# Two-layer graph and mixture-of-experts kernel: fillers of layer 0's table on SyncE, adjacency tiles held per pass, 25 pairs of pages in flight, four rounds of pages first

## The chip, the core and the metric

The kernel runs on one core of one Trainium2 chip. A core has five engines with a queue each: TensorE (PE, with its weight loads as PEld), VectorE (DVE), ScalarE (ACT), GpSimd (POOL) and SyncE (SP). SP computes nothing here: it issues DMAs. ACT and POOL issue some too. The metric is the device time of one execution in microseconds. Before the change it is 1949.97 us, the median of three runs (1948.76 to 1953.71).

## The reference

The input is x with 128 graphs of 64 nodes and 256 features, which is 8192 tokens, and an adjacency matrix of 64 x 64 for each graph. Two layers follow one another, each a graph step and a mixture of experts:

```python
x = x + _L0_gnn_ref(_layernorm(x, axis=-1), adj, ...)
x = x + _L0_ffn_ref(_layernorm(x, axis=-1), L0_ffn_gate_w, L0_ffn_lattice_weights, ...)
x = x + _L1_gnn_ref(_layernorm(x, axis=-1), adj, ...)
x = x + _L1_ffn_ref(_layernorm(x, axis=-1), L1_ffn_Wg, L1_ffn_W1, L1_ffn_W2, ...)
```

The part that matters here is the mixture of layer 0. Each token chooses 6 of 64 experts, an expert is one matrix of 256 x 256, and the token's answer is the sum of its six products, weighted by a softmax:

```python
logits = jnp.einsum('bsd,ed->bse', x, gate_w)
top_logits, indices = jax.lax.top_k(logits, TOP_K)      # TOP_K = 6
scores = jax.nn.softmax(top_logits, axis=-1)
xW = jnp.einsum('bsd,bskde->bske', x, lattice_weights[indices])
lattice_out = jnp.einsum('bske,bsk->bse', xW, scores)
```

Then follow a projection with `out_w`, a residual and a layer norm. Layer 1 multiplies the normed tokens by the adjacency again, and its mixture chooses 2 of 8 experts with a hidden layer of 512.

## The kernel before

Tokens are worked in 32 blocks of 256. There are four stages.

**First stage** (lines 775 to 1069). The graph step of layer 0 for each block, its routing, and a scatter of each token's six rows into a table in DRAM, `r0x`, in which each expert has chunks of its own (`Router.send`, line 419, an indirect DMA of POOL per 128 rows). A row carries 256 numbers, the place where its answer belongs, and its weight. `page_table` (line 443) then lists the pages: a page is 128 rows of one expert. Per expert the first `R` full pages come first, then the other full pages, then parts. The expert matrices, `lat`, are loaded in this stage too and fill 128 KB of each partition.

**Expert stage of layer 0** (lines 1073 to 1215). Twelve pages whose place is known early are done first (`early`). Then pages go in pairs: 188 pairs of listed pages, then 7 pairs whose pages are made of two halves of different experts. Three functions make a pair:

- `fetch(j)`, line 1138: SP loads two pages into `px`, of which there are `bufs=22`. A room comes free when the answers that were written over it have been scattered.
- `flip(j)`, line 1153: PE transposes into `pt` (line 1159), and ACT copies to `pxT` (line 1162).
- `apply(j)`, line 1173: for the first 64 pairs it first calls `r0.fill_end(j)`; then PE multiplies by the matrix (line 1188), DVE weighs the result into `px` (line 1192), and `reply` scatters it by an indirect DMA of POOL into `r0y` (line 426), one for each page.

`staggered` (line 658) sets the program order: a fetch stands 12 pairs ahead of the apply, a transpose 3 pairs ahead (2 for the first four and for the halves). PE, DVE and ACT follow the program order. SP's and POOL's queues are put in order by the framework's scheduler. The framework also has each DMA that SP or ACT issues wait for an earlier DMA on the same one of eight completion lanes.

The fillers: a filler is a page of rows without a token, written behind the last row of an expert so that a part page has defined rows (`fill_end`, line 613, `fill`, line 233; one DMA of 129 KB for each of 64 experts; every fourth call loads four row numbers into registers of the issuing engine). A page that is certainly full is read without waiting for any filler (`full_pages`, 309 pages; pairs from 154 on wait for all fillers).

**Third stage** (lines 1340 to 1667). For each block: the six answers of each token are loaded from `r0y` (`load_y`, line 1355, three rooms `y`), added up by PE (line 1382), projected, normed, and taken through the graph step of layer 1. `READY = 6`: `r0.look_back()` notes after block 5 how many rows each expert has, and `page_table` checks that these all lie in the first `R` pages; then `load_y` of blocks 0 to 5 needn't wait for the answers of later pages (the group `r0last`, which holds the replies from page `R * E` on). Otherwise the kernel runs its spare pages and a wait. `y` uses memory that `lat` leaves.

`load3` (line 1369) loads x and the adjacency of a block. The four adjacency tiles `at0` to `at3` are used in turn by the first and the third stage (`load_adjacency`, line 745). They live in the pool `const` for the whole kernel, 4 KB of each partition, and POOL zeroes them once.

**Fourth stage** (from line 1670). The experts of layer 1 over their pages; its fillers are issued by ACT through the same `fill_end`.

Of the kernel before, what the change touches and what calls it, by code (L numbers as in the profile page):

```python
# [19 lines left out]
P = 128  # L20
# [86 lines left out]
class Router:  # L107
# [502 lines left out]
                                       op0=ALU.add, op1=ALU.max)  # L610
        v.tensor_copy(self.total_pages, most)

    def fill_end(self, e):

        if e % 4 == 0:
            _, self.ends = self.nc.values_load_multi_w_load_instructions(
                self.last[0:1, e:e + 4], engines=[ENG.Activation], min_val=0, max_val=self.spare - self.pg,
                skip_runtime_bounds_check_because="the rows of an expert end in its chunk")
        self.fill(self.nc.scalar, self.ends[e % 4])

    def load(self, what, i, engine):

# [44 lines left out]
def two_layer_gnn_moe_kernel(ctx: ExitStack, tc: tile.TileContext, a: dict, out: bass.AP):  # L667
# [13 lines left out]
    K0 = 6  # L681
    E1, F1, _ = a["L1_ffn_W2"].shape
    EARLY = 12
    READY = 6
    FIRST = 4
    FOLD = 2
    LOOK = 20
# [49 lines left out]


    adjacency = []
    for i in range(4):  # L740
        at = const.tile([P, T, P], F32, name=f"at{i}")
        nc.gpsimd.memset(at, 0.0)
        adjacency.append(at)

    def load_adjacency(b):
        at = adjacency[b % 4]
        for g in range(2):
            nc.sync.dma_start(out=at[g * G:(g + 1) * G, :, g * G:(g + 1) * G],
                              in_=adjT[2 * b * T + g:2 * (b + 1) * T:2].rearrange("t m n -> m t n"))
        return at  # L750
# [24 lines left out]
    with tc.tile_pool(name="c0", bufs=1) as c0, \  # L775
            tc.tile_pool(name="work0", bufs=2) as work, \
            tc.tile_pool(name="ph0", bufs=4, space=PSUM) as ph_pool, \
            tc.tile_pool(name="ps0", bufs=2, space=PSUM) as psum, \
            tc.tile_pool(name="pm0", bufs=1, space=PSUM) as pmix:
        mean = c0.tile([P, P], F32, name="mean")  # L780
        nc.gpsimd.memset(mean, 1.0 / H0)
        route = pmix.tile([P, 2, T, E0], F32, name="route")
# [191 lines left out]
        aggregate(0)  # L974
        rest = lambda f: lambda b: f(b) if b else None

        r0 = Router(tc, const, small, dram, N, D, E0, K0, T, P, 14 * P, 4, "r0", 3, ((K0 * N // P - EARLY) // 4 * 4 + 4, E0 // 2 - 4), True)
        r1 = Router(tc, const, small, dram, N, D, E1, 2, T, 2 * P, N, 4, "r1", 1,
                    (N // P // 2 - E1 // 2, E1 // 4, E1 - 1), True, total=out, like=r0)
        assert W == r0.W  # L980
# [135 lines left out]
    with tc.tile_pool(name="wx0", bufs=3, reuse_waits="tile") as wx, \  # L1116
            tc.tile_pool(name="pt1", bufs=4, space=PSUM, reuse_waits="tile") as pt_pool, \
            tc.tile_pool(name="py1", bufs=4, space=PSUM, reuse_waits="tile") as py_pool:
        npair = (r0.pages + 1) // 2
        pairs = [dict(n=min(2, r0.pages - 2 * j), parts=1) for j in range(npair)]  # L1120
        pairs += [dict(n=2, parts=2) for j in range(E0 // 4)]
        regs = {}
        ring = [wx.tile([P, KD, C], F32, name="pxT", bufs=5)]
        over = dict(ln_g=r0.map.rearrange("p j e -> p (j e)")[:, :D], ln_b=r0.nth.rearrange("p j e -> p (j e)")[:, :D],
                    gamma=r0.end[:, :KD], beta=r0.delta[:, :KD], bg=r0.alloc[:, :E1], gbias=r0.none[:, :E1])

        def load_vectors(j):

            if 8 <= j < 14:
                name, v = (("ln_g", "L0_ffn_ln_g"), ("ln_b", "L0_ffn_ln_b"), ("gamma", "L1_gnn_ln_gamma"),  # L1130
                           ("beta", "L1_gnn_ln_beta"), ("bg", "L1_ffn_bg"), ("gbias", "L1_ffn_bias"))[j - 8]
                with nc.allow_non_contiguous_dma(reason="small vector"):
                    nc.scalar.dma_start(out=over[name], in_=a[v].rearrange("(c p) -> p c", p=P) if j in (10, 11)
                                        else rows_of(a[v]))
            if j == 18:
                nc.vector.tensor_add(over["bg"], over["bg"], over["gbias"])

        def fetch(j):
            Q = pairs[j]
            Q["px"] = px = wx.tile([P, 2, W], F32, name="px", bufs=22)  # L1140
            if j >= npair:
                regs["row"] = r0.load(2, 4 * (j - npair), ENG.SP)
                for i in range(4):
                    q, h = i // 2, i % 2 * P // 2
                    r0.fetch_rows(regs["row"][i], px[h:h + P // 2, q:q + 1, :], P // 2)
                return
            for q in range(Q["n"]):
                i = 2 * j + q
                if i % 4 == 0:
                    regs["row"] = r0.load(0, i, ENG.SP)  # L1150
                r0.fetch(i, regs["row"][i % 4], px[:, q:q + 1, :])

        def flip(j):
            Q = pairs[j]
            pt = pt_pool.tile([P, KD, C], F32, name="pt")
            n = Q["n"]
            for q in range(n):
                for k in range(KD):
                    nc.tensor.transpose(pt[:, k, ts(q, P)], Q["px"][:, q, ts(k, P)], ident)  # L1159
            if Q["parts"] == 1:  # L1160
                Q["xT"] = xT = ring.pop() if ring else wx.tile([P, KD, C], F32, name="pxT", bufs=5)
                nc.scalar.copy(xT[:, :, :n * P], pt[:, :, :n * P])  # L1162
                return
            Q["xT"] = []
            for q in range(n):
                xT = wx.tile([P, KD, C], F32, name="pxT", bufs=5)
                Q["xT"].append(xT)
                nc.vector.memset(xT[:, :, P // 2:P + P // 2], 0.0)
                for h in (0, 1):
                    nc.scalar.copy(xT[:, :, 3 * h * P // 2:3 * h * P // 2 + P // 2],  # L1170
                                   pt[:, :, q * P + h * P // 2:q * P + h * P // 2 + P // 2])

        def apply(j):
            Q = pairs[j]
            if j < E0:
                r0.fill_end(j)
            Q = pairs[j]
            if Q["parts"] == 2:
                regs["e"] = r0.load(3, 4 * (j - npair), ENG.PE)
            elif j % 2 == 0:  # L1180
                regs["e"] = r0.load(1, 2 * j, ENG.PE)
            py = py_pool.tile([P, 2, D], F32, name="py")
            px, xT, n, parts = Q["px"], Q["xT"], Q["n"], Q["parts"]
            for q in range(n):
                for h in range(parts):
                    e = regs["e"][2 * q + h if parts == 2 else (2 * j + q) % 4]
                    for k in range(KD):
                        nc.tensor.matmul(py[:, q, :], lhsT=xT[q][:, k, ts(h, P)] if parts == 2 else xT[:, k, ts(q, P)],  # L1188
                                         rhs=lat[:, ds(e, 1), k, :].rearrange("p o d -> p (o d)"),
                                         start=(h + k == 0), stop=(h == parts - 1 and k == KD - 1))  # L1190
            for q in range(n):
                nc.vector.tensor_scalar(px[:, q, :D], py[:, q, :], px[:, q, D + 1:D + 2], None, op0=ALU.mult)  # L1192
                r0.reply(2 * j + q, px[:, q, :], px[:, q, :D])


        stages = ((-12, fetch), (0, apply),
                  (-2, lambda j: flip(j) if j < 4 or j >= npair else None),
                  (-3, lambda j: flip(j) if 4 <= j < npair else None))

        def run(order, *more):  # L1200
            order = tuple(order)
            staggered(len(order), [*((lag, lambda n, f=f: f(order[n])) for lag, f in stages), *more])

        usual = r0.likely_pages // 2
        likely = (r0.likely_pages + E0 // 8) // 4 * 2
        ends = npair + r0.likely_halves // 4
        run((*range(usual), *range(npair, ends)), (0, load_vectors))
        wait = const.tile([1, 4], F32, name="wait")
        with tc.If(r0.needed(2 * usual)):
            run((*range(usual, likely), *range(ends, len(pairs))))  # L1210
            with tc.If(r0.needed(2 * likely)):
                run(range(likely, npair))

                nc.sync.dma_start(out=wait, in_=r0.answer[0:1, 0:4])
# [125 lines left out]
    with tc.tile_pool(name="c3", bufs=1, reuse_waits="tile") as c3, \  # L1340
# [5 lines left out]
        ln_g, ln_b, gamma, beta, bg = (over[x] for x in ("ln_g", "ln_b", "gamma", "beta", "bg"))  # L1346
        w_rel, w_root = (c3.tile([P, KD, D], F32, name="m_" + x) for x in ("rel", "root"))
        wg = load_matrix(c3, "L1_ffn_Wg")
        one = c3.tile([P, P], F32, name="one")
        nc.vector.memset(one, 1.0)  # L1350
        blocks = [dict() for _ in range(NB)]
# [44 lines left out]
        def fold(b):  # L1396

            B = blocks[b]
            B["n"] = K0
            if b > READY + 1:  # L1400
                B["n"] = n = K0 - FOLD
                y = B["y"]
                nc.vector.tensor_add(y[:, :, :FOLD], y[:, :, :FOLD], y[:, :, n:])
# [266 lines left out]
    with tc.tile_pool(name="pt4", bufs=2, space=PSUM, reuse_waits="tile") as pt_pool, \  # L1670
# [7 lines left out]
        def finish(i):  # L1678
            if i >= 0:
                what, m, new = listed(i)  # L1680
                if i < E1:
                    r1.fill_end(i)
                if new and not (what == 0 and i % 2):
                    regs["e", what] = r1.load(what + 1, m, ENG.PE)
            share(i)
# [61 lines left out]
```

## Time and profile before

| what | us |
|---|---|
| median of the runs | 1949.97 |
| the profiled execution | 1948.88 |
| its span, first to last instruction | 1947.1 |
| PE busy in the span | 1845.0 |
| POOL busy | 1134.5 |
| DVE busy | 1146.9 |
| ACT busy | 1001.6 |
| early answers' scatters on POOL begin | 614.9 |
| first px load, first px scatter | 619.4, 630.2 |
| PE's last product of the expert stage ends | 1097.6 |
| POOL's last scatter of the expert stage ends | 1131.4 |
| PE's last product of the kernel ends | 1931.0 |

Times within the span are counted from its first instruction. The page cuts the span into 40 slices of 48.7 us and gives a busy tenth for each. Windows give the same in stretches that one chooses, with the number of instructions in brackets. A timeline names each instruction with its start, its length, its line, what it writes and reads, and in square brackets the engine's idle time before it and what ended it. The engine's name with a q (SPq) is its queue: there a DMA's line shows its issue, not its transfer. The mean granted clock of PE over the span is 0.98.

### The profile page before, as it was taken

What the parts mean: (1) busy time and instruction counts of PE and PEld (TensorE: products, weight loads), DVE (VectorE), ACT (ScalarE), POOL (GpSimd) and SP (SyncE); (2) the same over time, 40 slices, a digit from 0 to 9 for tenths busy, and PEclk for the clock granted to TensorE, in tenths of its full rate; (3) what the DMA queues carried; (4) which work ended last, traced back from release to release, by engine and by line L of the source; (5) the groups of instructions that cost most, each with busy time, mean ns of one, the idle gap of its engine ahead of it and who ended that gap; (6) DMA issues with size and microseconds to landing.
All of it is one profiled execution on the core that took longest, in us unless ns stands there. A gap on an engine that the chain in (4) does not pass through costs nothing. (4 is left out here: it accounts for less than half of the span.)

```text
span 1947.1 us, 35284 instructions
## 1 busy us (share of the span) xinstructions
PE 1845.0 (95%) x9906; PEld 1608.8 (83%) x9906; DVE 1146.9 (59%) x4256; ACT 1001.6 (51%) x2047; POOL 1134.5 (58%) x1114
## 2 busy tenths in 40 slices
PE   7999999999966898999999899999999999999996
PEld 6888888888844787888887788888888888888885
DVE  5899999999976333344433279999974222222221
ACT  5888898889841222222222156666663333333332
POOL 1377777777677677777777734444454544444443
PEclk9999999999977999999999999999999999999998
DMA  5134555544376988766666689878626766656653
GB/s 141 62 132 144 165 162 164 162 152 137 122 251 193 305 265 263 227 210 204 210 208 201 234 325 328 300 262 287 212 101 139 167 143 127 142 125 141 123 108 44
DMA packets 253085, 359.49 MB, mean 185 GB/s; under 512 B 53176, under 2 KB 210504, under 8 KB 252880
## 3 DMA queue, kind: packets, MB, share of 16 engines
q1 hardware_dynamic: 175904, 210.74, 36.9%
q0 software_dynamic: 62736, 135.21, 23.5%
q10 hardware_dynamic: 14240, 11.12, 1.8%
q8 instruction: 90, 1.47, 0.3%
q14 instruction: 115, 0.94, 0.2%
HBM read 193.27 MB, written 166.03 MB: 185 GB/s over the span
## 5 line engine op out<-in xcount | busy, mean ns | idle before, releaser
L419 POOL DMA_INDIRECT r0x<-xs,r0row x384 | 388.5, 1012 | 215.1 <-ACT lat L883 112.5
L426 POOL DMA_INDIRECT r0y<-px x390 | 378.7, 971 | 122.9 <-issue 40.0
L1188 PE MATMUL py<-lat,pxT 128*128 x1616 | 387.0, 384 | 20.8 <-ACT pxT L1162 17.6
L436 POOL DMA_INDIRECT out_x<-px x131 | 202.8, 1548 | 265.9 <-DVE px L1333 173.7
L1192 DVE TENSOR_SCALAR px<-py,px 128x256 f32<-128x256 f32 x390 | 170.8, 480 | 304.6 <-PE py L1188 298.4
L1188 PEld LDWEIGHTS py<-lat,pxT 128*128 128x128 f32 x1616 | 294.0, 192 | 61.2 <-ACT pxT L1162 23.9
L1162 ACT COPY pxT<-pt 128x512 f32<-128x512 f32 x188 | 109.7, 585 | 346.5 <-PE pt L1159 242.4
L1294 ACT ACTIVATE phid<-ph,pw 128x256 f32<-128x256 f32 (+1 forms) x264 | 122.0, 462 | 287.8 <-PE ph L1285 181.0
L419 POOL DMA_INDIRECT r1x<-xs,r1row x128 | 135.0, 1054 | 179.6 <-ACT hn L1447 55.9
L894 PE MATMUL ps<-lat 128*128 128x256 f32 x1024 | 238.9, 382 | 0.0
L858 PE MATMUL ph<-lat 128*128 128x256 f32 x1024 | 231.5, 385 | 3.2 <-DVE lat L881 2.0
L1310 PE MATMUL py<-fw,phid 128*128 (+1 forms) x1016 | 230.4, 380 | 0.0
L1285 PE MATMUL ph<-pxT,pw 128*128 128x256 f32 (+1 forms) x1056 | 227.3, 368 | 1.5 <-DVE px L1327 1.5
L858 PEld LDWEIGHTS ph<-lat 128*128 128x128 f32 x1024 | 195.0, 193 | 29.6 <-issue 2.7
L894 PEld LDWEIGHTS ps<-lat 128*128 128x128 f32 x1024 | 193.7, 192 | 27.8
L1285 PEld LDWEIGHTS ph<-pxT,pw 128*128 128x128 f32 x1056 | 193.2, 190 | 26.3 <-DVE px L1327 1.9
L1310 PEld LDWEIGHTS py<-fw,phid 128*128 128x128 f32 x1016 | 188.2, 190 | 22.5
L1321 DVE TENSOR_SCALAR p<-p 128x2 f32<-128x2 f32 (+1 forms) x69 | 12.6, 183 | 208.0 <-ACT p L1320 208.0
L1159 PE MATMUL pt<-ident,px 128*128 128x128 f32 x780 | 121.4, 276 | 7.0 <-DMA px<-r0x 6.7
L1327 DVE TENSOR_TENSOR px<-py,pb 128x512 f32<-128x512 f32 (+1 forms) x67 | 44.5, 664 | 138.3 <-PE py L1310 133.7
L881 DVE SCALAR_TENSOR_TENSOR lat<-ph,c_L_gnn_b,rms 128x256 f32<-128x256 f32 x256 | 111.9, 477 | 23.3 <-ACT rms L72 23.3
L1159 PEld LDWEIGHTS pt<-ident,px 128*128 128x128 f32 x780 | 97.5, 142 | 31.5 <-DMA px<-r0x 6.2
(337 smaller groups left out, 2959.6 us busy)
## 6 DMA issues: line engine op xcount, KB each, us to landing
y<-r0y SPq DMA_DIRECT2D x64, 768.0 KB
px<-r0x SPq DMA_DIRECT2D x376, 129.0 KB
pw<-in_L_ffn_W1b SPq DMA_DIRECT2D x41, 514.0 KB
x<-x SPq DMA_DIRECT2D x64, 256.0 KB
px<-r1x SPq DMA_DIRECT2D x28, 516.0 KB
r0x<-r0filler ACTq DMA_DIRECT2D x64, 129.0 KB
lat<-in_x SPq DMA_DIRECT2D x32, 256.0 KB
lat<-in_L_ffn_lattice_weights SPq DMA_DIRECT2D x8, 1024.0 KB
```

What stands on the lines that cost most here:

```text
L419: i = self.nc.gpsimd.indirect_dma_start(out=self.table[:, :], out_offset=bass.IndirectOffsetOnAxis(ap=row[:, t, k:k + 1], axis=0), in_=xs[ ...
L426: d = self.nc.gpsimd.indirect_dma_start(out=self.answer[:, :], out_offset=bass.IndirectOffsetOnAxis(ap=x[:, self.D:self.D + 1].bitcast(I32 ...
L436: i, d = f"{self.name}add{i}", self.nc.gpsimd.indirect_dma_start(out=self.total[:, :], out_offset=bass.IndirectOffsetOnAxis(ap=x[:, self.D ...
L858: nc.tensor.matmul(ph[:, c, :], lhsT=w1[:, k, ts(2 * j + c, P)], rhs=B["aggT"][:, k, :], start=(k == 0), stop=(k == KD - 1))
L881: nc.vector.scalar_tensor_tensor(hT[:, c, :], B["ph", c // 2][:, c % 2, :], b1[:, c:c + 1], B["rms"], op0=ALU.add, op1=ALU.mult)
L894: nc.tensor.matmul(B["po"][:, t, :], lhsT=B["hT"][:, c, ts(t, P)], rhs=w2[:, c, :], start=False, stop=(t == T - 1 and c == KH - 1))
L1159: nc.tensor.transpose(pt[:, k, ts(q, P)], Q["px"][:, q, ts(k, P)], ident)
L1188: nc.tensor.matmul(py[:, q, :], lhsT=xT[q][:, k, ts(h, P)] if parts == 2 else xT[:, k, ts(q, P)], rhs=lat[:, ds(e, 1), k, :].rearrange("p ...
L1192: nc.vector.tensor_scalar(px[:, q, :D], py[:, q, :], px[:, q, D + 1:D + 2], None, op0=ALU.mult)
L1285: nc.tensor.matmul(Q["up", c][:, :m], lhsT=Q["w"][:, k * F1 + c * P:k * F1 + (c + 1) * P], rhs=Q["xT"][:, k, :m], start=(k == 0), stop=(k ...
L1294: nc.scalar.activation(Q["hid"][:, c, :m], Q["up", c][:, :m], AF.Relu, bias=Q["w"][:, KD * F1 + c:KD * F1 + c + 1], scale=1.0)
L1310: nc.tensor.matmul(py[:, t, :], lhsT=Q["hid"][:, c, ts(t, P)], rhs=fw2[:, ds(e, 1), c, :].rearrange("p o d -> p (o d)"), start=(c == 0), s ...
```

## The change

Five things are changed together:

1. Layer 0's fillers are issued by SP within `fetch`, at even pairs from 24 to 150 in program order, in place of ACT within `apply`. Layer 1's stay on ACT.
2. The four adjacency tiles are made twice, in a pool of the first stage (zeroed by POOL) and in a pool of the third (zeroed by DVE), and don't exist in between.
3. `px` has 25 rooms, not 22.
4. `R` of layer 0's router is 4, not 3, so that the list begins with up to four full pages of each expert, and `READY` is 8, not 6.
5. The test for adding up four products in place of six (`fold`) is written with a constant of its own; it is true for the same blocks as before.

```diff
-    def fill_end(self, e):
+    def fill_end(self, e, engine, issuer):
 
         if e % 4 == 0:
             _, self.ends = self.nc.values_load_multi_w_load_instructions(
-                self.last[0:1, e:e + 4], engines=[ENG.Activation], min_val=0, max_val=self.spare - self.pg,
+                self.last[0:1, e:e + 4], engines=[engine], min_val=0, max_val=self.spare - self.pg,
                 skip_runtime_bounds_check_because="the rows of an expert end in its chunk")
-        self.fill(self.nc.scalar, self.ends[e % 4])
+        self.fill(issuer, self.ends[e % 4])
...
-    READY = 6
+    READY = 8
+    WHOLE = 8
...
     adjacency = []
-    for i in range(4):
-        at = const.tile([P, T, P], F32, name=f"at{i}")
-        nc.gpsimd.memset(at, 0.0)
-        adjacency.append(at)
+
+    def clear_adjacency(pool, engine):
+        for i in range(4):
+            at = pool.tile([P, T, P], F32, name=f"at{i}")
+            engine.memset(at, 0.0)
+            adjacency.append(at)
 
     def load_adjacency(b):
-        at = adjacency[b % 4]
+        at = adjacency[b % 4 - 4]
...
+        clear_adjacency(c0, nc.gpsimd)
         mean = c0.tile([P, P], F32, name="mean")
...
-        r0 = Router(tc, const, small, dram, N, D, E0, K0, T, P, 14 * P, 4, "r0", 3, ((K0 * N // P - EARLY) // 4 * 4 + 4, E0 // 2 - 4), True)
+        r0 = Router(tc, const, small, dram, N, D, E0, K0, T, P, 14 * P, 4, "r0", 4, ((K0 * N // P - EARLY) // 4 * 4 + 4, E0 // 2 - 4), True)
...
         def fetch(j):
             Q = pairs[j]
-            Q["px"] = px = wx.tile([P, 2, W], F32, name="px", bufs=22)
+            if j % 2 == 0 and 24 <= j < 24 + 2 * E0:
+                r0.fill_end((j - 24) // 2, ENG.SP, nc.sync)
+            Q["px"] = px = wx.tile([P, 2, W], F32, name="px", bufs=25)
...
         def apply(j):
-            Q = pairs[j]
-            if j < E0:
-                r0.fill_end(j)
             Q = pairs[j]
...
         wg = load_matrix(c3, "L1_ffn_Wg")
+        clear_adjacency(c3, nc.vector)
...
-            if b > READY + 1:
+            if b >= WHOLE:
...
-                    r1.fill_end(i)
+                    r1.fill_end(i, ENG.Activation, nc.scalar)
```

## The prediction, made before the changed kernel was run

> **What bounds the kernel now.** I read the page's slices first, then twenty-microsecond windows over the expert stage of layer 0, then the timelines of GpSimd (POOL), TensorE (PE) and SyncE there. The page has PE busy 95% of the span, so the question is where the other 5% lies and who sets the time meanwhile.
>
> ```profile
> PE   7999999999966898999999899999999999999996
> POOL 1377777777677677777777734444454544444443
> ...
> L426 POOL DMA_INDIRECT r0y<-px x390 | 378.7, 971 | 122.9 <-issue 40.0
> ```
>
> PE's gaps are in slices 11 to 15 and in 22, counted from 0 (535 to 780 us and 1070 to 1120). The row L426 is the scatter of answers: 390 of them, each 0.97 us of POOL with about 0.30 us in front. The windows (columns: window; length; busy PE, PEld, DVE, ACT, POOL, each with its instruction count; clock; DMA share; GB/s):
>
> ```profile
> 640.00:660.00 20.00, 16.09 (x86) 13.37 (x84) 6.75 (x16) 3.60 (x7) 15.12 (x17) 1.00 0.97 312
> 660.00:680.00 20.00, 16.66 (x84) 13.55 (x84) 5.97 (x15) 4.22 (x8) 12.13 (x13) 1.00 0.96 288
> 880.00:900.00 20.00, 20.00 (x114) 17.70 (x112) 8.39 (x20) 5.34 (x10) 15.13 (x16) 1.00 0.70 210
> 1040.00:1060.00 20.00, 17.77 (x92) 14.16 (x91) 7.01 (x16) 4.38 (x8) 15.26 (x16) 1.00 0.68 209
> 1100.00:1120.00 20.00, 13.57 (x83) 12.03 (x84) 3.22 (x11) 2.79 (x5) 15.38 (x16) 0.83 1.03 398
> 1140.00:1160.00 20.00, 20.00 (x137) 18.06 (x136) 14.52 (x72) 13.21 (x29) 2.81 (x3) 1.00 0.94 322
> ```
>
> A pair of pages is twelve PE instructions (four transposes, eight products). At 112 to 114 per 20 us PE needs 2.14 us for a pair; POOL needs two scatters at a spacing of 1.275 us, 2.55 us. So POOL is the slower one through the whole stage and PE runs ahead of it. From about 995 us PE falls to 92 to 98 instructions per 20 us, 2.6 us for a pair: POOL's pace. It can't get further ahead, since a room of px comes free only when its scatter has landed, and there are 22. The stage's ends:
>
> ```profile
> 664.63 0.97 POOL L426 DMA_INDIRECT r0y<-px  x1 [0.30 <-issue]
> 667.16 0.97 POOL L426 DMA_INDIRECT r0y<-px  x1 [1.57 <-DMA px<-r0x]
> ...
> 670.48 0.97 POOL L426 DMA_INDIRECT r0y<-px  x1 [1.07 <-DVE px L1192]
> ...
> 678.75 0.97 POOL L426 DMA_INDIRECT r0y<-px  x1 [2.21 <-DMA px<-r0x]
> ...
> 1130.47 0.97 POOL L426 DMA_INDIRECT r0y<-px  x1 [0.31 <-issue]
> 1137.11 0.76 POOL L366 TENSOR_SCALAR xs<-r1dest 128x4 int32<-128x4 f32 x3 [5.67 <-DMA r0y<-px]
> ...
> 1090.51 7.07 PE L1188 MATMUL py<-lat,pxT 128*128 x32
> 1103.22 2.79 PE L1382 MATMUL ps<-ident,y 128*128 128x128 f32 x12 [5.64 <-DMA y<-r0y]
> ...
> 1097.73 0.85 SPq L1359 DMA_DIRECT2D y<-r0y  x2
> ```
>
> POOL's queue has only three holes after its first px scatter at 630.20, all at 665 to 680, together 4.85 us where 0.90 is usual: 3.95 us lost. 630.20 + 390 x 1.275 = 1127.5, plus 3.95 is its measured end, 1131.4. PE ends its pairs at 1097.6, 34 us before POOL. Only then does the first load of y start, 0.15 us later: y lies where the matrices were, so it waits for PE, not for POOL. From about 1126 PE has no hole worth a name until the last page. **So the end of the kernel hangs on when PE leaves the pairs, 1097.6, plus a ramp of 28.6 us in which DMA is full (1.03) and PE idles 10.3 us.** POOL counts only as the pacemaker that holds PE back before that.
>
> **What the Trainium skill says.** "Perfetto Trace Analysis", section Optimization Strategy: a gap that repeats on the engine that should be saturated can mean too few buffers for the next tile. The trace agrees (92 instead of 113 instructions per 20 us with waits for px). "DMA: Bandwidth & Descriptors", section Issuing engines are not separate DMA queues: DMAs of SP, ACT and POOL share 16 engines, so another issuer saves only its own queue's time. The trace agrees: with fillers the share is 0.86 to 0.97, without 0.70, whoever issues. The same page, section Why small descriptors are slow, puts a fixed overhead on packets of 256 bytes; the adjacency rows are 256 bytes. No view here isolates them; I price them by a neighbour below.
>
> **Part by part.** The reference point is the profiled execution: 1948.88 us, of which the span is 1947.1; the median of the runs is 1949.97, 1.1 above.
>
> Fillers. In before each sits in ACT's queue ahead of the copy that PE waits for, and shares DMA completion lanes with the px loads (by the listed order, each of SP's or ACT's DMAs waits for an earlier one on its lane, eight issues back where lanes go round). So the px loads can't outrun ACT. That is what holds PE at 84 to 86 instructions at 640 to 680 and opens POOL's holes. What leaves ACT: 64 issues of 0.34 us and 16 register loads of 0.31, 26.7 us, none on the path by itself. What SP takes is the same: per pair it has two loads of 0.33 us, half a table load of 0.31 and at most 0.42 for a filler, about 1.3 of 2.55 us. The order of the built program is not quite the source's: SP issues fillers 0 to 2 ahead of the last part of the matrices and the first px load, fillers 3 to 11 at every second pair up to pair 46, and the other 52 one per pair, pairs 47 to 99. Those fall to about 690 to 820 us. Before ran the same density at 680 to 780 at a DMA share of 0.86 to 0.94 with POOL full, and here PE has a lead by then. Value: POOL's 3.95 us come back. Bounds: 0 (the three early fillers or the dense stretch open holes of the same size) and 3.95 (there are no others).
>
> Three more px rooms. PE's lead at the start of its last seven pairs (1070.4; these take it 3.9 us each, since each page is applied twice): POOL has (1131.4 - 1070.4)/1.275 = 48 scatters left, 24 pairs, PE seven: a lead of 17 out of 22 rooms. The five others are scatter landing, load and transposes made three pairs ahead. With 25 the lead is 20. PE reaches it in time: 20 x 2.55/0.41 = 124 pairs, about 890 us. So PE leaves the pairs three POOL pairs earlier: 7.65 us. Bounds: 5.1 (one of three eaten by slower landings) and 7.65.
>
> Together PE leaves at 1097.6 - 7.65 - 3.95 = 1086.0, POOL at 1127.5.
>
> Four rounds and READY 8. Block 6 of y waits for all scatters in before, block 8 now; its load would come at about 1136 (1146.9 - 11.6 and a little), POOL's landings at about 1133 (1127.5 and the 5.7 us that L366 waited). No stall, so nothing is gained or lost by itself; without this, block 6's load (1134.7 less 11.6) would wait about 10 us of a slack of some 20 (issued 1137, used 1155). The inputs' routing leaves at least 105 rows of margin in the test that sends the kernel into its spare pages, so these aren't run.
>
> Adjacency per pass. In before SP loads the tiles of blocks 0 to 3 of layer 1 at the end of the first stage. Now they come between the loads of x and y in the ramp: eight DMAs of 0.60 us issue (1.25 for two), 128 packets each. By bytes: 0.26 MB at the ramp's 379 GB/s, 0.7 us. By packets: the ramp's ACT queue had 544 packets for 3.3% of 16 engines in 29 us, 28 ns each, so 1024 are 1.8 us. By issue, all serial: 4.8 us. I take 2.0, range 0 to 4.8; below nothing only through fewer waits of SP before 560, which POOL's queue of sends (unbroken from 540) hides. Four memsets of 0.30 us go to DVE, which idles 17.3 us there: nothing.
>
> Sum: -3.95 - 7.65 + 2.0 = **-9.6 us**: 1939.3 for a profiled execution, 1940.4 as the median. What is late next is the ramp: y's bytes.
>
> **Rivals.**
> 1. The holes of POOL stay or move (for: DMA is at 0.97 in the burst of first loads, and three fillers stand ahead of it; against: they leave while SP waits for the last sends): -7.65 + 2.0, 1944.3.
> 2. The lead doesn't count because the ramp waits for POOL after all (for: block 8 of y still waits for every scatter, and scatters run 13 us beyond the ramp instead of 5, in a stretch at 0.94; against: some 3 us of slack plus three buffers): -3.95 + 2.0, 1948.0.
> 3. Slower, by one mechanism: the adjacency pairs in SP's queue during the ramp. Each waits for its lane, that is for one of the y or x loads eight issues earlier, and holds up the y load behind it. If a pair costs a landing rather than its issue (first y: 5.5 us), four are 4 x 4.2 = 17 us beyond what is overlapped: -11.6 + 17, 1955. It decides from 2.9 us a pair on (11.6/4). Against: before's y loads wait for lanes of the same age.
>
> **Chances.** Forecast 0.70, rivals 0.12, 0.10 and 0.08. Bounds of the forecast: 1937 (adjacency free and a shorter ramp) to 1945. The range, 1935.5 to 1947.5, covers it and rival 1, and leaves out most of rivals 2 and 3. Faster by over 0.3% (5.85 us; about what a measurement of this kernel can tell) is under 1944.1: 0.67 from the forecast and half of rival 1, 0.73. Within: 0.17, most of rival 2 and what is left of the first two. Slower: 0.10, rival 3 and a fifth of rival 2.
>
> **What will show it.** Right: POOL without holes from 630 to 1127.5; PE at 112 per 20 us from 640 to about 890, then 94; its last L1188 product ending near 1086 with 41 us of scatters left; the first product on y 5 to 6 us later; PE full from about 1117. Wrong: waits of POOL for px around 630 or 690 to 820; a y load that waits for scatters; holes of PE in the ramp over 15 us with SP waiting at adjacency loads.

## The result, and the profile after

| | before | after |
|---|---|---|
| median of six executions each | 1949.25 us | 1938.53 us |
| the profiled execution | 1948.88 | 1939.37 |
| PE leaves the pairs of the expert stage | 1097.58 | 1085.82 |
| from there to the end of that execution | 851.30 | 853.55 |
| POOL's last scatter of the expert stage ends | 1131.4 | 1127.1 |

The ratio is 0.9943 with a 95% interval of [0.9931, 0.9956]: 10.7 us faster by the medians, 9.5 us by the two profiled executions. A ratio compares only those executions of a kernel that lie within 1.5% of its fastest, so it need not be the ratio of the medians. The third and fourth rows do the book-keeping of all that follows: the time of an execution is "PE leaves" (the end of PE's last product of the expert stage) plus "the rest", and the change made the first 11.76 us smaller and the second 2.25 us larger.

The busy slices and the groups, from the page of the kernel after (the new line 1191 is the old line 1188):

```profile
PE   7999999999966999999999799999999999999996
POOL 1267777777777777777777734444454544444443
...
L426 POOL DMA_INDIRECT r0y<-px x390 | 379.0, 972 | 119.0 <-DMA r0y<-px 45.8
L1191 PE MATMUL py<-lat,pxT 128*128 x1616 | 386.4, 384 | 5.1 <-DVE px L1195 2.8
```

PE's slices 13 and 15 (within 630 to 775 us) had 8 and now have 9. POOL's scatters cost what they did, 0.97 us each. The windows that the prediction shows, in the kernel after (window; length; busy PE, PEld, DVE, ACT and POOL with their instruction counts; clock; DMA share; GB/s):

```profile
640.00:660.00 20.00, 20.00 (x112) 17.66 (x111) 7.89 (x18) 4.28 (x8) 15.19 (x16) 1.00 0.92 300
660.00:680.00 20.00, 19.98 (x110) 17.35 (x109) 7.96 (x19) 6.25 (x11) 15.36 (x16) 1.00 0.90 281
880.00:900.00 20.00, 18.57 (x103) 15.90 (x102) 7.71 (x18) 4.89 (x9) 15.12 (x17) 1.00 0.67 201
1040.00:1060.00 20.00, 17.51 (x89) 13.86 (x88) 8.10 (x20) 4.47 (x13) 15.33 (x16) 1.00 0.62 192
1100.00:1120.00 20.00, 16.93 (x107) 14.72 (x106) 10.21 (x35) 7.00 (x14) 15.40 (x16) 0.94 1.02 373
```

In the first two, PE's count rose from 86 and 84 to 112 and 110, and POOL's busy time at 660 to 680 from 12.13 to 15.36 us: nothing holds either of them there now. At 880 to 900 PE is already slowing (103 against 114): it has used up its rooms. From 880 to 1060 us it waits for px loads, and SP, which issues them, waits 73.7 us for scatters to land. The timelines of POOL and PE at the end of the stage:

```profile
1126.14 0.97 POOL L426 DMA_INDIRECT r0y<-px  x1 [0.30 <-DVE bn_st L56]
1133.80 0.61 POOL L366 TENSOR_SCALAR xs<-r1dest 128x4 int32<-128x4 f32 x3 [6.69 <-DMA r0y<-px]
```

```profile
1078.75 7.07 PE L1191 MATMUL py<-lat,pxT 128*128 x32
1091.31 2.79 PE L1386 MATMUL ps<-ident,y 128*128 128x128 f32 x12 [5.48 <-DMA y<-r0y]
...
1115.45 1.53 PE L1386 MATMUL ps<-ident,y 128*128 128x128 f32 x12 [1.05 <-DMA y<-r0y]
```

PE leaves at 1078.75 + 7.07 = 1085.82 with 41.3 us of scatters still ahead of POOL (before: 34). POOL's queue has no hole over 0.45 us between its first px scatter (629.47) and its last. PE's last hole of the ramp is at 1115.45. Its holes between 1085.82 and there add up to 11.2 us, against 10.4 before (the prediction read 10.3). And the ramp in SP's queue, where the adjacency now is:

```profile
1086.26 0.82 SPq L1363 DMA_DIRECT2D y<-r0y  x2
...
1089.13 1.07 SPq L1363 DMA_DIRECT2D y<-r0y  x2
...
1093.44 2.92 SPq L751 DMA_DIRECT2D at<-in_adjT  x2
1096.41 1.06 SPq L1363 DMA_DIRECT2D y<-r0y  x2
...
1099.56 3.31 SPq L751 DMA_DIRECT2D at<-in_adjT  x2
1103.29 0.80 SPq L1363 DMA_DIRECT2D y<-r0y  x2
...
1106.18 3.76 SPq L751 DMA_DIRECT2D at<-in_adjT  x2
1110.63 1.30 SPq L1363 DMA_DIRECT2D y<-r0y  x2
...
1112.85 3.18 SPq L751 DMA_DIRECT2D at<-in_adjT  x2
1116.36 0.80 SPq L1363 DMA_DIRECT2D y<-r0y  x2
...
1123.92 1.26 SPq L751 DMA_DIRECT2D at<-in_adjT  x2
```

The same loads of y, the third to the sixth, in the kernel before:

```profile
1106.34 0.96 SPq L1359 DMA_DIRECT2D y<-r0y  x2
...
1109.11 0.80 SPq L1359 DMA_DIRECT2D y<-r0y  x2
...
1114.83 0.80 SPq L1359 DMA_DIRECT2D y<-r0y  x2
...
1121.25 0.90 SPq L1359 DMA_DIRECT2D y<-r0y  x2
```

A pair of adjacency loads holds SP's queue for 2.9 to 3.8 us in the ramp, not for the 1.25 us that two issues take behind it (the last line of the kernel after). Counted from the moment PE leaves, the third to sixth loads of y are issued at 10.6, 17.5, 24.8 and 30.5 us; in the kernel before it was 8.8, 11.5, 17.3 and 23.7.

### The profile page after: what moved, and what is told of

Read it like the earlier page. It is cut to its first block, busy times and chain, and to the rows that moved or that the text cites. A ratio compares the mean times of both kernels' runs of the same rounds, so it can differ in the third digit from the quotient of the medians.

```text
span 1937.6 us, 35277 instructions
## 1 busy us (share of the span) xinstructions
PE 1845.5 (95%) x9906; PEld 1610.8 (83%) x9906; DVE 1147.9 (59%) x4260; ACT 1001.6 (52%) x2047; POOL 1136.1 (59%) x1114
## 5 line engine op out<-in xcount | busy, mean ns | idle before, releaser
L426 POOL DMA_INDIRECT r0y<-px x390 | 379.0, 972 | 119.0 <-DMA r0y<-px 45.8
L419 POOL DMA_INDIRECT r1x<-xs,r1row x128 | 135.7, 1060 | 170.8 <-ACT hn L1451 48.7
```

The lines of the kernel that those rows point to most:

```text
L419: i = self.nc.gpsimd.indirect_dma_start(out=self.table[:, :], out_offset=bass.IndirectOffsetOnAxis(ap=row[:, t, k:k + 1], axis=0), in_=xs[ ...
L426: d = self.nc.gpsimd.indirect_dma_start(out=self.answer[:, :], out_offset=bass.IndirectOffsetOnAxis(ap=x[:, self.D:self.D + 1].bitcast(I32 ...
```

## The experiments

The theory: POOL's scatters pace the expert stage, a hole (idle time) in POOL's queue is lost for good, each px room lets PE leave one POOL pair (2.55 us) earlier, and the end follows when PE leaves plus a ramp that the adjacency makes a little longer. Each part of the change but the constant of `fold` was tried alone or taken back, and then versions that the theory said should be faster. Unless said otherwise an edit is made to the kernel after.

### The rooms taken back

```diff
-            Q["px"] = px = wx.tile([P, 2, W], F32, name="px", bufs=25)
+            Q["px"] = px = wx.tile([P, 2, W], F32, name="px", bufs=22)
```

> The changed kernel with 22 rooms for px in place of 25, all else kept. Theory (the end follows PE's leave of the expert stage, and PE's lead over POOL is the rooms): POOL's last scatter still ends at about 1127, PE's last product of the stage ends three POOL pairs later, at 1085.8 + 7.65 = 1093.5, and the profiled time is 1939.4 + 7.65 = 1947.0. Rival (the fillers' move is all of the gain): PE still leaves near 1086 and the time stays at 1939.

Measured: 1946.7 us, ratio to before 0.9983 [0.9976, 0.9989]; profiled 1945.69. The timeline of PE:

```profile
1086.33 7.07 PE L1191 MATMUL py<-lat,pxT 128*128 x32
```

PE leaves at 1093.40, 7.58 us later than with 25 rooms, while POOL's last scatter ends at 1127.10, where it did (1127.11). Three rooms are three pairs of POOL, and they move PE alone. This is the larger half of the gain.

### The fillers back on ACT

```diff
         def fetch(j):
...
-            if j % 2 == 0 and 24 <= j < 24 + 2 * E0:
-                r0.fill_end((j - 24) // 2, ENG.SP, nc.sync)
...
         def apply(j):
             Q = pairs[j]
+            if j < E0:
+                r0.fill_end(j, ENG.Activation, nc.scalar)
```

> The changed kernel with layer 0's fillers issued by ScalarE in apply again, one per pair for 64 pairs, all else kept. Theory: PE drops to 84 to 98 instructions per 20 us between 640 and 800, POOL gets holes of about 4 us between 650 and 700, POOL and PE end the stage about 4 us later (1131 and 1090), time 1943. Rival (only the rooms count): POOL has no holes, time 1939.

Measured: 1945.04 us, 0.9973 [0.9964, 0.9982]; profiled 1945.49. POOL's timeline and a window of this kernel:

```profile
671.83 0.97 POOL L426 DMA_INDIRECT r0y<-px  x1 [1.70 <-DVE px L1195]
...
680.18 0.97 POOL L426 DMA_INDIRECT r0y<-px  x1 [2.20 <-DVE px L1195]
```

```profile
660.00:680.00 20.00, 14.58 (x75) 11.62 (x73) 5.55 (x14) 3.72 (x7) 12.64 (x13) 1.00 0.95 299
```

The holes are back, at the same place, and PE falls to 75 instructions. They cost 1.70 + 2.20 - 2 x 0.30 = 3.3 us. PE leaves 5.9 us later than after (1091.72): 3.3 are the holes, and the other 2.6 stand before the stage, since the first px scatter began at 632.10 and not at 629.47. SP's last load of the matrices was already 2.6 us late (613.89 against 611.28), before this kernel issues any filler; the run doesn't say what delayed it.

### READY and the rounds taken back

```diff
-    READY = 8
+    READY = 6
...
-        r0 = Router(tc, const, small, dram, N, D, E0, K0, T, P, 14 * P, 4, "r0", 4, ((K0 * N // P - EARLY) // 4 * 4 + 4, E0 // 2 - 4), True)
+        r0 = Router(tc, const, small, dram, N, D, E0, K0, T, P, 14 * P, 4, "r0", 3, ((K0 * N // P - EARLY) // 4 * 4 + 4, E0 // 2 - 4), True)
```

> The changed kernel with three rounds of pages first and READY 6 as before, all else kept. Theory: block 6 of y is loaded only when all scatters have landed, at about 1133 in place of 1125, but is used at about 1145, so PE has no new hole and the time stays at 1939 (+-1). Rival (four rounds carry part of the gain): a hole of PE in front of block 6's sums, up to 10 us, time up to 1949.

Measured: 1938.91 us, 0.9945 [0.993, 0.996], from four executions; profiled 1936.47. The kernel after has 0.9943. No effect of this part is seen, with an interval of about 3 us to either side. Its PE:

```profile
1076.25 7.07 PE L1191 MATMUL py<-lat,pxT 128*128 x32
```

PE leaves at 1083.32; the rest is 853.15.

### The fillers alone, in the kernel before

The kernel before with the diff's edits to `fill_end` and its calls: the two lines in `fetch`, and none in `apply`. It keeps the constant adjacency tiles, 22 rooms and three rounds.

> The kernel before with only the fillers moved to SyncE's fetch; 22 rooms, adjacency in const, three rounds, READY 6. Theory: POOL without holes, its last scatter at 1127.5, PE leaves at 1093.6, the ramp as before, profiled time 1948.9 - 4.0 = 1944.9. Rival (PE's faster start counts as such): PE's 22 us of idle at 640 to 800 come off, PE leaves at 1075 and the time is near 1927.

Measured: 1945.57 us, 0.9979 [0.9972, 0.9986]; profiled 1946.3. PE's and POOL's timelines:

```profile
1087.26 7.07 PE L1187 MATMUL py<-lat,pxT 128*128 x32
```

```profile
1126.62 0.97 POOL L426 DMA_INDIRECT r0y<-px  x1 [0.30 <-issue]
```

POOL had no hole and PE left at 1094.33, 3.25 us earlier than in the kernel before; 1.18 of this was there at the first px scatter (629.02 against 630.20). The rest is 851.97. By the medians of the same chip the gain is 4.3 us (1949.84 before).

### The adjacency alone, and three variants, on a chip with a lower clock

The next four ran on a chip that granted PE 0.92 to 0.93 of its clock on the mean, where the kernel before takes 2276.35 us; their times can only be compared with that. The kernel before with the adjacency per pass alone (the diff's edits to `load_adjacency` and the two calls of `clear_adjacency`):

> The kernel before with only the adjacency tiles made per pass (and SP's loads of blocks 0 to 3 so moved into the ramp). Theory: PE leaves the expert stage where it did (1097.6, +-1.5 with the first stage), the time from there to the end grows from 851.3 by 1.6 to 2.3 us, profiled time 1950.5 to 1951.2. Rival (it costs nothing, SP and DMA have room): 1948.9. Rival (each pair of loads costs a landing): 1960.

The adjacency of blocks 0 to 3 issued by ACT, in `load_weights` (`load_adjacency` is given the issuing engine):

```diff
-    def load_adjacency(b):
+    def load_adjacency(b, engine=None):
...
         def load_weights(b):
+            if 0 <= b < 4:
+                blocks[b]["at"] = load_adjacency(b, nc.scalar)
...
-            B["at"] = load_adjacency(b)
+            if b > 3:
+                B["at"] = load_adjacency(b)
```

> The changed kernel with the adjacency of layer 1's blocks 0 to 3 loaded by ScalarE's queue, outside SP's order of y loads; everything else kept. Theory (SP's order and lanes cost the ramp about 2 us): PE's leave stays at 1086, the time from there to the end falls from 853.6 to about 851.5, profiled time 1937.3. Rival (the bytes and packets cost it, whoever issues): 1939.4.

The seven half pairs, which take PE 3.9 us each, run 32 pairs before the end and not last:

```diff
-        run((*range(usual), *range(npair, ends)), (0, load_vectors))
+        ahead = usual - 32
+        run((*range(ahead), *range(npair, ends), *range(ahead, usual)), (0, load_vectors))
```

> The changed kernel with the seven pairs of half pages worked 32 pairs before the end of the list and not last. These take PE 3.9 us each where POOL needs 2.55. Theory (the end follows PE's leave, and PE idles for rooms from 890 us on): PE regains the lead that these pairs cost, so it leaves 20 pairs ahead of POOL's end and not 16: about 1076 in place of 1085.8, POOL's end unchanged at 1127; profiled time about 1930. Rival (POOL's end holds the ramp): block 8 of y waits for scatters, PE gets holes behind block 7, time 1935 to 1939.

The fillers by SP at every pair from 12 on, as dense and early as ACT's had been:

```diff
-            if j % 2 == 0 and 24 <= j < 24 + 2 * E0:
-                r0.fill_end((j - 24) // 2, ENG.SP, nc.sync)
+            if 12 <= j < 12 + E0:
+                r0.fill_end(j - 12, ENG.SP, nc.sync)
```

> The changed kernel with SP issuing one filler per pair from pair 12 on in program order, so that the fillers fall in the same time as in the kernel before, but not on ScalarE's queue. Theory (ScalarE's filler in front of the copy makes POOL's holes): no holes, time 1939 as with the change. Rival (the fillers' bytes in the burst of first loads make them): holes of about 4 us between 650 and 700, time 1943.

Measured, in this order: 2274.96, 2269.81, 2273.41 and 2277.67 us; ratios 0.9994 [0.9964, 1.0023], 1.0027 [0.9989, 1.0065], 0.9984 [0.9956, 1.0012] and 0.9999 [0.997, 1.0027]. None differs from the kernel before beyond its interval, and none of the theories is told apart. Why the parts count for so little there is read from the run with the dense fillers repeated on a second such chip (below). The second and third of these four were run again on a chip that granted 0.98.

### The half pairs before the end, again

> The changed kernel with the seven pairs of half pages worked 32 pairs before the end of the list and not last, once more, on a chip that grants TensorE its full clock. Theory (the end follows PE's leave, and PE idles for rooms from 890 us on): PE regains the lead that these pairs cost, leaves 20 pairs ahead of POOL's end and not 16, about 1076 in place of 1085.8, POOL's end unchanged at 1127; profiled time about 1930. Rival (POOL's end holds the ramp): block 8 of y waits for scatters, PE gets holes behind block 7, time 1935 to 1939.

Measured: 1930.19 us, 0.9900 [0.9885, 0.9915]; profiled 1930.47. This version is faster than both kernels, by 8.3 us than the kernel after. Its PE and POOL:

```profile
1069.92 5.35 PE L1191 MATMUL py<-lat,pxT 128*128 x24
1082.27 2.79 PE L1387 MATMUL ps<-ident,y 128*128 128x128 f32 x12 [6.99 <-DMA y<-r0y]
```

```profile
1127.75 0.98 POOL L426 DMA_INDIRECT r0y<-px  x1 [0.30 <-DMA r0y<-px]
```

With the halves last, PE spends seven pairs slower than POOL and gives back 7 x (3.9 - 2.55) = 9.4 us of its lead at the worst place. Run earlier, they cost the same, and the 32 usual pairs behind them can win it back (32 x 0.41 = 13 us). PE leaves at 1075.27, 10.55 earlier, and POOL ends at 1128.73, 1.6 later. That PE's leaving sets the end, and not POOL's, is shown most plainly here; but 1.65 of the 10.55 were lost again (the rest is 855.2), nearly all in the wait for the first y (6.99 us against 5.48).

### The adjacency on ACT's queue, again

> The changed kernel with the adjacency of layer 1's blocks 0 to 3 loaded by ScalarE's queue, outside SP's order of y loads, once more. Theory (SP's order and lanes cost the ramp about 2 us): PE's leave stays at 1086, the time from there to the end falls from 853.6 to about 851.5, profiled time 1937.3. Rival (the bytes and packets cost it, whoever issues): 1939.4.

Measured: 1940.74 us, 0.9955 [0.9942, 0.9969]; profiled 1941.6, PE leaves at 1086.56, the rest is 855.04. No gain where one of about 2 us was hoped for. PE and SP's queue of this run:

```profile
1079.49 7.07 PE L1191 MATMUL py<-lat,pxT 128*128 x32
...
1086.91 2.39 SPq L1363 DMA_DIRECT2D y<-r0y  x2
1092.31 0.40 SPq L1373 DMA_DIRECT2D m_rel<-in_L_gnn_W_rel  x1
...
1096.58 0.81 SPq L1363 DMA_DIRECT2D y<-r0y  x2
```

SP issues no adjacency for these blocks any more, and yet its second load of y is at 1096.58, 7.45 us later than in the kernel after, where PE left only 0.74 earlier. So taking the adjacency out of SP's order wins nothing back, and the rival, that the bytes and packets cost it whoever issues, fits better than the theory. What SP's queue waited for at 1080 to 1140 us (us in total, times, longest), first in the kernel after and then in this run:

```profile
SPq L751 <- DMA y<-r0y: 11.1, 7, 2.5
```

```profile
SPq L1363 <- DMA at<-in_adjT: 6.3, 3, 2.4
```

No adjacency load needs y, and no load of y needs the adjacency. They wait for each other's landing all the same, which fits the completion lanes that all DMAs of SP and ACT share. How much the lanes add to what the full DMA engines take anyway isn't told apart.

### One room more, and the dense fillers again

The half pairs early, `px` with 26 rooms, and `pxT` with four buffers for the memory:

```diff
-        ring = [wx.tile([P, KD, C], F32, name="pxT", bufs=5)]
+        ring = [wx.tile([P, KD, C], F32, name="pxT", bufs=4)]
...
-            Q["px"] = px = wx.tile([P, 2, W], F32, name="px", bufs=25)
+            Q["px"] = px = wx.tile([P, 2, W], F32, name="px", bufs=26)
```

> The changed kernel with the half pairs run 32 pairs before the end of the stage, a twenty-sixth px room and pxT with four buffers in place of five (memory holds no fifth beside the room). Theory (rooms set how far TensorE is ahead of GpSimd): one more room is one more pair of 2.55 us, TensorE leaves the pairs near 1072.7 (1075.3 with 25 rooms), GpSimd's last scatter still ends at 1127 to 1128, profiled time 1927.9, median about 1927.6. Rival A: pxT with four buffers makes TensorE wait for its copies, or the lead isn't reached in time: TensorE leaves near 1075 or later, 1930 or more. Rival B: the ramp already waits for GpSimd's scatters or for DMA: TensorE leaves near 1072.7, but the time stays at about 1930.

> The changed kernel with SyncE's fillers twice as dense and earlier: one at every pair from 12 to 75 of the program order, so that they fall in the burst of first px loads, as ScalarE's did before the change. Theory (a filler in ScalarE's queue ahead of TensorE's copy made the holes of GpSimd's queue): SyncE's queue has room, no hole over 1 us, TensorE leaves near 1086, median about 1939. Rival (the filler's bytes and its place in the burst made the holes, whoever issues): GpSimd loses 3 to 4 us between 630 and 700, TensorE leaves near 1090, median about 1943. An earlier try on a chip with a lower clock could not tell them apart.

Both ran on another chip, and it too granted only 0.93: 2273.4 and 2276.63 us where the kernel before takes 2281.54; ratios 1.0028 [0.9975, 1.0081] and 1.0052 [1.0015, 1.009]. The medians say a little faster and the ratios a little slower, so no order can be read from either run. Both questions stay open: whether a twenty-sixth room is worth 2.55 us more, and whether it was ACT's queue or the early, dense bytes of the fillers that opened POOL's holes. In the first run PE left at 1415.09, 11.8 us ahead of POOL's end, so it can have been only four to five pairs ahead with 26 rooms. Its rest was 859.95, 6 us above the others: SP's first load of y came 6.75 us after PE's last product and not 0.44 as in the kernel after, and the run doesn't show why. What the second run does show is why such a chip can't answer. The slices and the group of scatters from its page, a window, and lines of its POOL and PE timelines:

```profile
PE   7978879888887367787887788899999999999997
...
PEclk9988989999888578899999999999999999999999
...
L426 POOL DMA_INDIRECT r0y<-px x390 | 379.4, 973 | 230.9 <-DVE px L1195 104.6
```

```profile
940.00:980.00 40.00, 33.27 (x164) 27.99 (x163) 10.93 (x26) 7.39 (x14) 25.74 (x27) 0.91 0.62 186
```

```profile
945.39 0.97 POOL L426 DMA_INDIRECT r0y<-px  x1 [2.26 <-DVE px L1195]
...
1429.08 7.07 PE L1191 MATMUL py<-lat,pxT 128*128 x32
...
1438.23 0.98 POOL L426 DMA_INDIRECT r0y<-px  x1 [0.30 <-DVE at L745]
```

PE does 164 instructions in 40 us, 2.9 us for a pair of twelve, slower than POOL's 2.55. POOL waits for it again and again: 230.9 us ahead of its scatters, where the kernel after has 119.0, most of that the usual 0.30 between two. PE leaves at 1436.15 and POOL ends at 1439.2, 3 us later and not 41: PE has hardly any lead, so neither rooms nor single holes of POOL count.

## Why the prediction was right

The predicted 1940.4 us was 1.9 above the median, and the profiled execution came out at 1939.37 where the sum gave 1939.3. That the latter two agree within 0.1 us is in part luck: 0.73 of the 11.76 us were there at the first px scatter, which in the runs with SP's fillers on chips of the higher clock came anywhere from 628.14 to 630.60. By the medians, each against the kernel before on its own chip, the fillers alone gave 4.3 us, all but the rooms 3.1, and the whole change 10.7: 4.3 for the fillers, 7.6 for the rooms, and 1.1 lost to the adjacency with the rounds.

- **What bounds.** That the end follows PE's leaving and not POOL's last scatter is shown by the rooms (PE 7.6 us later and POOL unmoved: 6.3 us slower in the profiled execution) and by the early halves (PE 10.55 earlier, POOL 1.6 later: 8.9 faster).
- **Fillers, 3.95.** Their holes closed entirely. Alone they brought PE 3.25 us forward in the profiled execution and the median down by 4.3; taken back they cost 3.3 in holes, and 2.6 more that stood before the stage and aren't explained. So the term was right to within 0.7, that delay apart. That three early fillers or the dense stretch at 690 to 820 would open new holes didn't happen (from 700 to 800, windows have 112 to 115 PE instructions at a DMA share of 0.85 to 0.89). Rival 1 is out. That a filler ahead of a copy in ACT's queue is the mechanism remains argued: the move changed the issuer, the place and the density together.
- **Rooms, 7.65.** Measured 7.58. The Trainium skill, "Perfetto Trace Analysis", section Optimization Strategy, says that a gap which keeps repeating on the engine that should be saturated can mean too few buffers; it names the cause, and its price here was POOL's 2.55 us for each room. The lead was reached somewhat before 890 us, as the 103 instructions at 880 to 900 tell.
- **PE's leaving at 1086.0 and POOL's end at 1127.5.** Measured 1085.82 and 1127.11. The first product on y followed 5.48 us later, and PE was full after 1117.
- **READY and rounds, 0.** No effect was measured: with READY 6 and 25 rooms there is no loss beyond the interval either, which fits the slack of block 6 that the prediction spoke of. Rival 2, that the ramp waits for POOL, is out: then rooms would not have moved the end.
- **Adjacency, 2.0.** The size was about right; whether the working was isn't shown. The prediction priced packets on a full DMA; the ramp shows waits of DMAs for one another besides, and no run takes the two apart. The Trainium skill, "DMA: Bandwidth & Descriptors", section Issuing engines are not separate DMA queues, says that DMAs run on the same 16 engines whoever issues them, so that another issuer saves only the time of issuing. The run with the adjacency on ACT agrees: it gained nothing (a rest of 855.04 against 853.55), and in the first 32 us after PE left the DMA share was 0.98 in both. The prediction wrote "whoever issues" of a trace in which ACT alone issued fillers; the kernel after, with SP, bears it out (0.92 and 0.90 at 640 to 680 us, where it was 0.97 and 0.96).
- **Rival 3.** It put a pair of adjacency loads at 4.2 us beyond what is overlapped, and was to decide from 2.9 on. The pairs did wait. Beyond the 1.25 us of issue the four held SP for 1.7 to 2.5 us each, 8.2 together where it had 17, and the sixth load of y slipped by 6.9 us against PE's leaving. Yet PE's holes grew only from 10.4 to 11.2 us, and the rest by 2.25. So rival 3 had the waits about twice too long, and charged them to PE in full. That three rooms of y and a DMA that was full anyway took up most of them is likely, and not shown apart; where the rest lost the 1.4 us that the holes don't account for isn't known.

What the adjacency cost can be read in two ways. The rests of the profiled executions are 851.30 and 851.97 with constant tiles, and 853.55 (after), 852.29 (22 rooms), 853.77 (fillers on ACT) and 853.15 (READY 6) with tiles per pass, a difference of the means of 1.6. And two runs on one chip, all of the change but the rooms and the fillers alone, differ only in the adjacency and in the rounds, which had no effect: 1946.7 against 1945.57 us by the medians of 21 and 19 executions, 1.1, and only 0.3 in their rests. The part alone was tried only where PE had hardly any lead.

Put together, tiles per pass cost about 1 to 2 us and free 4 KB of each partition in the expert stage, and a px room (2 x 258 numbers of 4 bytes) takes 2.1 KB and brings 2.5 us.

## What to carry to other kernels

Where one engine paces a stage and the end waits for another, buffers between them are worth one period of the slow engine each, as long as the fast one has the time to fill them. This is to be read as the lead in the slow engine's queue when the fast one leaves. A stretch in which the fast one is slower than the pacemaker belongs well before the end of the stage, not at it. A wait in a queue that feeds the start of the next stage isn't its cost: compare the idle time of the engine that the ramp feeds before charging it. And a gain that rests on one engine being slower than another goes when their speeds change, so the granted clock is read before the times are.

## What was not expected of the hardware

On the chips with a granted clock of 0.93, 5% below the others, the kernel before took 17% longer. No profile of that kernel was kept there. In the profile shown last, of the change with the dense fillers, nearly all of it lay in the first two stages: the first px scatter came at 831.62 us (629.47 after the change on the other chip), PE left at 1436.15, and from there to the end it was 852.1 us, much as on the other chips. So the loss isn't spread as the mean clock suggests: in the slices above the clock falls to 5 tenths in slice 13 (743 to 800 us), the one in which PE is busy 3 tenths, and is at 9 from slice 17 on. Which of the two is the cause of the other, the runs don't show.
